# Both ends of a three-part transformer block: two blocks normalized on ScalarE, ternary weights by quarters, and first products placed in the end of attention

## The chip, the cores and the metric

The kernel runs on one core of a Trainium2 chip. The metric is device time in microseconds (us), the median of several runs. The engines are TensorE (PE for products, PEld for its weight loads), VectorE (DVE), ScalarE (ACT), GpSimd (POOL) and the DMA queues (SP and ACT issue here). Each engine works through its own instructions in order; it waits on semaphores for the others.

## The reference

Sixteen sequences of 256 tokens, 256 features: 4096 tokens. A feed-forward network with ternary weights, attention, and the same network again, each behind a layer norm without scale:

```python
def _bit_quant(w):
    scale = jnp.maximum(jnp.mean(jnp.abs(w)), EPS)
    w_ternary = jnp.clip(jnp.round(w / scale), -1.0, 1.0)
    ...
h = jnp.einsum('bsd,fd->bsf', x, w1q) + b1
h = jax.nn.gelu(h, approximate=False)
return jnp.einsum('bsf,df->bsd', h, w2q) + b2
...
x = x + 0.5 * _L0_ffn_ref(_layernorm(x, axis=-1), ...)
x = x + _L0_attn_ref(_layernorm(x, axis=-1), ...)      # 16 heads of 16, RoPE, causal softmax
x = x + 0.5 * _L0_ffn_ref(_layernorm(x, axis=-1), ...)
```

The ternary weight of w is 1 where w is above half the mean size, -1 where it is below minus half of it, else 0. So the thresholds need the whole matrix (its mean size), and the signs need the thresholds.

## The kernel before

All of x stays in SBUF: eight blocks of four tiles of 128 tokens (BT = 4, TB = 512). Every compute instruction goes through a wrapper (line 167) that keeps the order in which the program writes them on each engine, so this order is the schedule. A tile pool with a number of buffers makes an instruction that writes a buffer wait until all users of its last content are done, also those that are written further down.

**Feed-forward network.** ffn(ln, after) is used twice, with ln = 0 in front of attention and ln = 2 behind it. Its step(u) takes block i and feature slice f (128 of 1024 features) from u = 8 i + f. up(i, f) makes four products of 512 columns (the input is split into a high and a rest part, two halves of the 256 features each), then two Gelu passes on ACT (h_high, rounded, and h_whole, exact) and a subtraction h_rest on DVE, or on POOL where f is 1, 3 or 5. down(i, f) comes two steps later (LATE = 2): eight products into the block's output in PSUM. So PE's order is: up(u), then, in some steps, a turning of the next block, then down(u-2). prepare(i) normalizes a block (xn, one buffer), turn_in(i, k) transposes half of its features on PE, copies it to a rounded high part on ACT, and subtracts on DVE; both are written into the steps of the block before (f = 3, and f = 5 and 6).

**The start** (ln = 0, begin, lines 352 to 364): measure(0) takes the statistics of block 0 on DVE, finish_stats makes 1/sqrt(var) on POOL with a power; sizes(0) sums the sizes of w1, one half on DVE and one on ACT; prepare(0) normalizes on DVE; threshold(0) averages over the partitions with a product on PE and makes two thresholds on DVE; signs(0, half) makes ternary weights of half of w1 in two DVE instructions of 1024 elements; then turn_in(0, k), the other half of w1, and sizes(1) for w2, both halves on ACT. Step 0 makes w2's threshold and the first half of its signs, step 3 the second half; step 1 takes the statistics of block 1, step 3 normalizes it on DVE.

**Attention.** slot(b, p) is one of eight places of sequence b. In each place scores() makes, for two heads, eight products for the weights of sequence b-1 (tile w, in PSUM, two buffers) and eight for the row maxima of sequence b (tile m, maxima on DVE). weigh() adds the mask on DVE and takes the exponential on ACT into pT (five buffers). Other work is hung between: attend(b, half) multiplies pT with the values (32 products) and ACT copies the sums out; divide turns them back, turn_out transposes, project_out makes the output product, add_out adds to x, last_stats takes the statistics for the second network. turn_max(b, j) puts the row maxima in place with two small DMAs from SP's queue.

**The end of attention** (lines 733 to 771, a = 14, z = 15): eight places with the scores of the last sequence alone; `ahead` is put between a place's products and its mask, `behind` after its exponential. The first product of the second network is up(0, 0) in the loop behind. What is left of sequence 15 is `tail`, one part after each of the first five steps.

PSUM is full: two buffers of two banks for w and the network's output (ps_w), two of one bank for m and up's result (ps_m), two of one bank for all else (ps_mm, tiles mm).

Of the kernel before, what the change touches and what calls it, by code (L numbers as in the profile page):

```python
# [8 lines left out]
FP = mybir.dt.float32  # L9
FR = mybir.dt.float32r  # L10
AF = mybir.ActivationFunctionType
ALU = mybir.AluOpType
# [17 lines left out]
def kernel(  # L30
# [24 lines left out]
    fp = ctx.enter_context(tc.tile_pool(name="ffn", bufs=2))  # L55
    pp = ctx.enter_context(tc.tile_pool(name="proj", bufs=2))
    hp = ctx.enter_context(tc.tile_pool(name="heads", bufs=2))
    prp = ctx.enter_context(tc.tile_pool(name="probs", bufs=5))

# [148 lines left out]
    def sizes(n):  # L208
        for k in range(2):
# [4 lines left out]
            else:  # L214
# [58 lines left out]
    def ffn(ln, after):  # L273
        xn, xnT, hT, ys = {}, {}, {}, {}

        def measure(i):
            if ln == 0:
                for t in range(BT):
                    stats(0, i * BT + t)
                finish_stats(0, i * BT, BT)  # L280

        def prepare(i, engine=None):
            xn[i] = fp.tile([P, BT, D], FP, name="xn", bufs=1)
            for t in range(BT):
                normalize(ln, i * BT + t, xn[i][:, t, :], engine)
            xnT[i] = [fp.tile([P, KC, TB], FR, name=f"xnT_{n}") for n in range(2)]

        def add_bias(i):
# [9 lines left out]
            scalar.copy(high, tp)  # L298
            return lambda: vector.tensor_sub(rest, tp, high.bitcast(FP))

        def up(i, f):
            h = ps_m.tile([P, TB], FP, name="m")
            for n in range(2):
                for k in range(KC):
                    tensor.matmul(
                        h,
                        w1q[:, k, f * P : (f + 1) * P],
                        xnT[i][n][:, k, :],
                        start=(n == 0 and k == 0),
                        stop=(n == 1 and k == KC - 1),  # L310
                    )
            high = fp.tile([P, TB], FR, name="h_high", bufs=LATE + 3)
            rest = fp.tile([P, TB], FR, name="h_rest", bufs=LATE + 3)
            whole = fp.tile([P, TB], FP, name="h_whole", bufs=3)
            scalar.activation(high, h, AF.Gelu, bias=b1_sb[:, f : f + 1])
            scalar.activation(whole, h, AF.Gelu, bias=b1_sb[:, f : f + 1])

            engine = gpsimd if f in (1, 3, 5) and not (ln == 0 and i == NBLK - 1) else vector
            engine.tensor_sub(rest, whole, high.bitcast(FP))
            hT[i, f] = (high, rest)  # L320

        def down(i, f):
# [20 lines left out]
            if f == NFC - 1:  # L343
# [5 lines left out]
                for t in range(0, BT, 2):  # L349
                    after(i, t)  # L350

        def begin():
            measure(0)
            if ln == 0:
                sizes(0)
            prepare(0)
            if ln == 0:
                threshold(0)
                signs(0, lambda w: w[:, :, 0 : FF // 2])
            for k in range(KC):  # L360
                turn_in(0, k)()
            if ln == 0:
                signs(0, lambda w: w[:, :, FF // 2 :])
                sizes(1)

        def step(u):
            i, f = divmod(u, NFC)
            if i < NBLK:
                up(i, f)
                if ln == 0 and u == 0:  # L370
                    threshold(1)
                if ln == 0 and u in (0, 3):
# [6 lines left out]
                if ln == 0 and f >= 4 and i + 2 < NBLK:  # L379
# [3 lines left out]
                if i + 1 < NBLK:  # L383
                    if f == 3:
# [3 lines left out]
                if f == (1 if i == NBLK - 1 else 6):  # L388
# [8 lines left out]
        return begin, step, prepare, turn_in  # L397

    FFN_STEPS = NBLK * NFC + LATE

# [157 lines left out]

        return weigh if w is not None else lambda: None

    def attend(b, half):
# [14 lines left out]
        sums[b, half] = pp.tile([P, 2, S], FP, name="avs")  # L576
        scalar.copy(sums[b, half], av)

    def divide(b, half):
# [59 lines left out]
    def slot(b, p, more=lambda: None):  # L639
# [90 lines left out]

    begin, step, prepare, turn_in = ffn(2, store)
    rest = []
    for p in range(8):
        made = []
# [84 lines left out]
```

## Time and profile before

| | us |
|---|---|
| median of three runs (625.16 to 626.89) | 625.42 |
| the profiled execution | 622.22 |
| its span, first to last instruction | 620.4 |
| PE busy / DVE / ACT / POOL | 599.5 / 461.2 / 416.3 / 300.9 |
| first product on PE | 8.22 |
| first product of up(0, 0), ln = 0 | 11.75 |
| first product of down(0, 0), ln = 0 | 18.12 |
| down(0, 3), behind the first turning of block 1 | 25.35 |
| first place with sequence 15 alone | 468.46 |
| last exponential begins | 483.48 |
| up(0, 5), ln = 2 | 495.66 |

Times inside the profile are counted from the span's start. A group of instructions of one kind is printed in one line with its start, its length from the first start to the last end, and its number; the square bracket says how long the engine had been idle before and which engine's instruction let it go. A product's own time overlaps the next one's, so what a group costs PE is the distance from its start to the start of the next.

In the steady part of a network four up products take 0.93 us and eight down products 0.93 us, 1.87 us a step.

### The profile page before, as it was taken

How to read it: one execution, taken by the hardware profiler on the slowest of the kernel's cores; microseconds unless marked ns; L12 is line 12 of the kernel's file. 1: busy time of each engine (PE TensorE's matmuls, PEld its weight loads, DVE VectorE, ACT ScalarE, POOL GpSimd, SP SyncE). 2: the span in 40 equal slices, each digit the busy share in tenths (PEclk: the TensorE clock that was granted, in tenths of full speed). 3: DMA queues.
4: the chain of work that ended last, by engine and by line, in shares of the span. 5: the costliest groups of instructions: out<-in, count | busy, mean ns of one | idle time of the engine just before them, and what ended most of it. 6: DMA issues, size and time to landing. Idle time of an engine off the chain costs nothing.

```text
span 620.4 us, 14716 instructions
## 1 busy us (share of the span) xinstructions
PE 599.5 (97%) x5580; PEld 486.6 (78%) x5580; DVE 461.2 (74%) x1654; ACT 416.3 (67%) x716; POOL 300.9 (49%) x273
## 2 busy tenths in 40 slices
PE   4999999999999999999999999999998999999997
PEld 3798999887667777777777777777766798888886
DVE  6877777786788888888888888888886465555553
ACT  4666766664576677676777677767765676676674
POOL 3655555782464455545564456453430243334443
PEclk9999999999999999999999999999999999999999
DMA  8800000000001000100001000100100011011001
GB/s 285 180 22 1 2 1 18 17 1 18 20 35 38 19 21 36 38 27 29 19 36 38 20 20 36 37 20 21 36 4 2 1 35 35 34 35 35 27 21 55
DMA packets 25478, 21.30 MB, mean 34 GB/s; under 512 B 10944, under 2 KB 21056, under 8 KB 25408
## 3 DMA queue, kind: packets, MB, share of 16 engines
q1 hardware_dynamic: 24848, 19.44, 9.8%
q8 instruction: 44, 0.72, 0.5%
q10 hardware_dynamic: 560, 0.92, 0.4%
q14 instruction: 26, 0.21, 0.1%
HBM read 7.51 MB, written 4.19 MB: 19 GB/s over the span
## 4 chain that ended last, share of the span: by engine, by line
PE 89%; DVE 5%; ACT 3%; issue 1%; DMA 1%; POOL 1%; DVEq 0%; SPq 0%; POOLq 0%
PE mm L167 38%; PE w L167 29%; PE m L167 22%; DMA w<-in_w1T_dram 1%; DVE h_rest L167 1%; DVE xn L167 1%; ACT h_high L167 1%; ACT h_whole L167 1%; DVE w2q L167 1%; DVE st L167 1%; DVE w L167 0%; DVE x L167 0%; DVE masked L167 0%; DVE mv L167 0%; ACT pT L167 0%
## 5 line engine op out<-in xcount | busy, mean ns | idle before, releaser
L167 DVE CUSTOM_DVE_ANT_0 masked<-m,mask_q 128x128 f32<-128x128 f32 x480 | 142.7, 354 | 41.0 <-PE m L167 39.7
L167 PE MATMUL m<-xnT,w1q 128*128 128x512 f32 x512 | 145.1, 404 | 0.8 <-ACT xnT L167 0.7
L167 ACT ACTIVATE h_high<-m,b_sb 128x512 fp32r<-128x512 f32 x128 | 88.5, 691 | 78.2 <-PE m L167 78.1
L167 DVE TENSOR_TENSOR h_rest<-h_whole,h_high 128x512 fp32r<-128x512 f32 x83 | 75.0, 904 | 72.0 <-ACT h_whole L167 71.5
L167 ACT ACTIVATE pT<-w 128x768 f32<-128x768 f32 x128 | 104.1, 815 | 31.4 <-DVE w L167 24.9
L167 PE MATMUL w<-qT,kT 32*128 32x256 f32 (+1 forms) x1024 | 120.6, 348 | 1.9 <-ACT pT L167 1.8
L167 PE MATMUL w<-w2q,h_high 128*128 128x256 f32 x480 | 120.8, 285 | 0.7 <-DVE w2q L167 0.7
L167 PE MATMUL w<-w2q,h_rest 128*128 128x256 f32 x480 | 117.8, 279 | 0.4 <-POOL h_rest L167 0.3
L167 PEld LDWEIGHTS w<-qT,kT 32*128 32x128 f32 x1024 | 89.9, 184 | 33.0 <-issue 25.9
L167 PE MATMUL m<-kT,qT 32*128 32x128 f32 x960 | 114.9, 349 | 0.7 <-ACT kT L167 0.7
L167 POOL TENSOR_TENSOR h_rest<-h_whole,h_high 128x512 fp32r<-128x512 f32 x45 | 60.1, 1335 | 108.5 <-ACT h_whole L167 108.4
L167 PEld LDWEIGHTS m<-xnT,w1q 128*128 128x128 f32 x512 | 88.3, 190 | 16.7 <-DVE xnT L167 2.9
L167 PEld LDWEIGHTS w<-w2q,h_rest 128*128 128x128 f32 x480 | 90.4, 188 | 5.1 <-POOL h_rest L167 0.7
L167 PEld LDWEIGHTS w<-w2q,h_high 128*128 128x128 f32 x480 | 90.3, 188 | 5.2 <-DVE w2q L167 1.2
L167 DVE TENSOR_TENSOR w<-w,mask_k 128x512 f32<-128x512 f32 x128 | 88.8, 695 | 7.1 <-PE w L167 7.0
L167 ACT ACTIVATE h_whole<-m,b_sb 128x512 f32<-128x512 f32 x128 | 87.3, 682 | 0.0
L167 PEld LDWEIGHTS m<-kT,qT 32*128 32x128 f32 x960 | 65.9, 185 | 2.9 <-ACT kT L167 1.6
L167 POOL TENSOR_TENSOR w<-w,cosT 128x512 f32<-128x512 f32 x32 | 41.3, 1292 | 51.8 <-ACT w L167 31.9
L167 PE MATMUL mm<-xnT_a,wqk 128*128 128x256 f32 x256 | 62.2, 386 | 0.0
L167 POOL TENSOR_SCALAR var<-mv 128x4 f32<-128x4 f32 (+1 forms) x32 | 6.9, 216 | 106.2 <-DVE mv L167 105.6
L167 POOL TENSOR_TENSOR w<-w,sinT 128x512 f32<-128x512 f32 x32 | 41.0, 1280 | 26.0 <-DMA w<-w 25.9
L167 PEld LDWEIGHTS mm<-xnT_a,wqk 128*128 128x128 f32 x256 | 46.1, 190 | 7.6 <-issue 0.7
(86 smaller groups left out, 918.9 us busy)
## 6 DMA issues: line engine op xcount, KB each, us to landing
w<-w SPq DMA_DIRECT2D x64, 128.0 KB
out_dram<-x SPq DMA_DIRECT2D x15, 256.0 KB
x<-in_x_dram SPq DMA_DIRECT2D x7, 512.0 KB
w<-in_w2T_dram SPq DMA_DIRECT2D x1, 1024.0 KB
qT<-mT SPq DMA_DIRECT2D x64, 4.0 KB
w<-in_w1T_dram SPq DMA_DIRECT2D x1, 512.0 KB
w<-in_w1T_dram ACTq DMA_DIRECT2D x1, 512.0 KB
wqk<-in_wqkvT_dram SPq DMA_DIRECT2D x16, 32.0 KB
```

The costliest lines, as they stand in the source:

```text
L167: return tc.keep_in_program_order(getattr(self.engine, name)(*args, **kwargs))
```

## The change

1. **Pools.** pT has six buffers for five.
2. **Start, normalizing.** prepare(0) and prepare(1) of the first network run on ACT as Identity with scale rstd and bias `less` = -mean * rstd, which two small POOL instructions make. prepare(1) moves from step 3 to step 4, behind the last statistics of block 1.
3. **Start, signs.** Signs are made by quarters (512 elements) in place of halves. begin makes two quarters of w1; threshold(1) and w2's first quarter move into up(0, 0), between its Gelus and its subtraction; the other five quarters come in steps 1 to 5 (table `soon`), and between them the statistics of block 1, one tile each in steps 1 to 4.
4. **Start, PE.** turn_on(n) makes n products of the 128x128 matrix `averaging` with itself, that nothing uses: 20 in front of sizes(0), 4 behind the turning of block 0.
5. **Statistics of block 2** go from steps 4 to 7 to steps 8 and 9; the bias of block 0 is added at f = 7 instead of 6.
6. **End of attention.** up is split: up_first makes its products, up the rest. project_out(13) and add_out(13) move from the last slot into place 0; the other parts move to later places; block 1 of the second network is normalized on POOL in place 1 and turned in places 6 and 7; the products of up(0, 0) and up(0, 1) stand in places 3 and 5, those of up(0, 2) and up(0, 3) behind place 7, in a buffer of ps_w.
7. **Tail.** attend(15, 1) leaves its sums in PSUM; the copy comes one step later.

```diff
-    prp = ctx.enter_context(tc.tile_pool(name="probs", bufs=5))
+    prp = ctx.enter_context(tc.tile_pool(name="probs", bufs=6))
...
+    def turn_on(n):
+        on = ps_m.tile([P, P], FP, name="m")
+        for _ in range(n):
+            tensor.matmul(on, averaging, averaging, start=True, stop=True)
...
         def prepare(i, engine=None):
...
+            if engine is scalar:
+                less = small.tile([P, BT], FP, name="less")
+                gpsimd.tensor_scalar(less, mv[ln][:, at, 0], -1.0, 0.0, ALU.mult, ALU.add)
+                gpsimd.tensor_mul(less, less, rstd[ln][:, at])
...
+                    scalar.activation(
+                        xn[i][:, t, :],
+                        tokens(n),
+                        AF.Identity,
+                        bias=less[:, t : t + 1],
+                        scale=rstd[ln][:, n : n + 1],
+                    )
...
-        def up(i, f):
-            h = ps_m.tile([P, TB], FP, name="m")
+        first = {}
+
+        def up_first(i, f, to=None):
+            h = first[i, f] = ps_m.tile([P, TB], FP, name="m") if to is None else to
             for n in range(2):
                 for k in range(KC):
                     tensor.matmul(
...
+        def up(i, f):
+            if (i, f) not in first:
+                up_first(i, f)
+            h = first.pop((i, f))
...
             scalar.activation(whole, h, AF.Gelu, bias=b1_sb[:, f : f + 1])
+            if ln == 0 and (i, f) == (0, 0):
+                threshold(1)
+                signs(1, quarter(1, 0))
...
+        def quarter(n, k):
+
+            at = slice(2 * k * P, 2 * (k + 1) * P) if n == 0 else slice(2 * k, 2 * (k + 1))
+            return (lambda w: w[:, :, at]) if n == 0 else (lambda w: w[:, at, :])
...
+        soon = {
+            1: ((1, 1), 0),
+            2: ((0, 2), 1),
+            3: ((0, 3), 2),
+            4: ((1, 2), 3),
+            5: ((1, 3), None),
+        }
...
         def begin():
             measure(0)
-            if ln == 0:
-                sizes(0)
-            prepare(0)
-            if ln == 0:
-                threshold(0)
-                signs(0, lambda w: w[:, :, 0 : FF // 2])
+            turn_on(20)
+            sizes(0)
+            prepare(0, scalar)
+            threshold(0)
+            signs(0, quarter(0, 0))
             for k in range(KC):
                 turn_in(0, k)()
-            if ln == 0:
-                signs(0, lambda w: w[:, :, FF // 2 :])
-                sizes(1)
+            turn_on(4)
+            signs(0, quarter(0, 1))
+            sizes(1)
...
-                if ln == 0 and u == 0:
-                    threshold(1)
-                if ln == 0 and u in (0, 3):
-                    part = slice(0, NFC // 2) if u == 0 else slice(NFC // 2, NFC)
-                    signs(1, lambda w: w[:, part, :])
+                if ln == 0 and u in soon:
+                    part, t = soon[u]
+                    if u == BT:
+                        stats(0, BT + t)
+                        finish_stats(0, BT, BT)
+                        prepare(1, scalar)
+                    signs(part[0], quarter(*part))
+                    if u < BT:
+                        stats(0, BT + t)
...
-                if u == 1:
-                    measure(1)
...
+                if ln == 0 and u in (NFC, NFC + 1):
+
+                    for t in range(0, BT, 2):
+                        stats(0, 2 * BT + t + u - NFC)
+                    if u == NFC + 1:
+                        finish_stats(0, 2 * BT, BT)
...
-            if last is not None:
+            if last is not None and b < NB - 1:
                 project_out(last)
...
+    def take_sums(b, half):
+        av, sums[b, half] = sums[b, half], pp.tile([P, 2, S], FP, name="avs")
         scalar.copy(sums[b, half], av)
...
-    add_out(NB - 3)
     ahead = {
-        0: lambda: turn_max(z, 1),
-        6: lambda: project_out(a),
+        0: lambda: project_out(NB - 3),
+        1: lambda: turn_max(z, 1),
     }
     behind = {
-        0: lambda: attend(a, 1),
-        4: lambda: turn_out(a),
-        5: lambda: attend(z, 0),
-        2: lambda: (divide(a, 1), last_stats(NB - 3)),
-        7: lambda: (add_out(a), last_stats(a), divide(z, 0)),
+        0: lambda: add_out(NB - 3),
+        1: lambda: prepare(1, gpsimd),
+        2: lambda: attend(a, 1),
+        3: lambda: up_first(0, 0),
+        4: lambda: (divide(a, 1), last_stats(NB - 3)),
+        5: lambda: (up_first(0, 1), attend(z, 0)),
+        6: lambda: (turn_out(a), turn_in(1, 0)()),
+        7: lambda: (turn_in(1, 1)(), project_out(a), add_out(a), divide(z, 0), last_stats(a)),
     }
...
+    more = ps_w.tile([P, 2, TB], FP, name="w")
+    for f in range(2):
+        up_first(0, 2 + f, more[:, f, :])
     tail = [
-        lambda: attend(z, 1),
+        lambda: attend(z, 1, False),
+        lambda: take_sums(z, 1),
         lambda: divide(z, 1),
```

More of the change, by code (lines that the diff above doesn't have):

```diff
@@ L283, in prepare @@
             xn[i] = fp.tile([P, BT, D], FP, name="xn", bufs=1)
-            for t in range(BT):
-                normalize(ln, i * BT + t, xn[i][:, t, :], engine)
+            at = slice(i * BT, (i + 1) * BT)
+            if engine is scalar:
+                less = small.tile([P, BT], FP, name="less")
+                gpsimd.tensor_scalar(less, mv[ln][:, at, 0], -1.0, 0.0, ALU.mult, ALU.add)
+                gpsimd.tensor_mul(less, less, rstd[ln][:, at])
+            for t in range(BT):
+                n = i * BT + t
+                if engine is scalar:
+                    scalar.activation(
[5 more added lines that the diff above has]
+                    )
+                else:
+                    normalize(ln, n, xn[i][:, t, :], engine)
             xnT[i] = [fp.tile([P, KC, TB], FR, name=f"xnT_{n}") for n in range(2)]
@@ L369, in step @@
                 up(i, f)
-                if ln == 0 and u == 0:
-                    threshold(1)
-                if ln == 0 and u in (0, 3):
-                    part = slice(0, NFC // 2) if u == 0 else slice(NFC // 2, NFC)
-                    signs(1, lambda w: w[:, part, :])
+                if ln == 0 and u in soon:
[7 more added lines that the diff above has]
+                        stats(0, BT + t)
                 if ln == 0 and u == 4:
                     gpsimd.tensor_scalar(b2_sb, b2_sb, 0.5, 0.0, ALU.mult, ALU.add)
-                if u == 1:
-                    measure(1)
-                if ln == 0 and f >= 4 and i + 2 < NBLK:
+                if ln == 0 and u in (NFC, NFC + 1):
[3 more added lines that the diff above has]
+                        finish_stats(0, 2 * BT, BT)
+                if ln == 0 and f >= 4 and 0 < i and i + 2 < NBLK:
                     stats(0, (i + 2) * BT + f - 4)
@@ L382, in step @@
                         finish_stats(0, (i + 2) * BT, BT)
-                if i + 1 < NBLK:
-                    if f == 3:
+                if i + 1 < NBLK and (ln, i) != (2, 0):
+                    if f == 3 and (ln, i) != (0, 0):
                         prepare(i + 1)
@@ L387, in step @@
                         turn_in(i + 1, f - 5)()
-                if f == (1 if i == NBLK - 1 else 6):
+                if f == (1 if i == NBLK - 1 else 7 if ln == 0 and i == 0 else 6):
                     add_bias(i)
@@ L395, in step @@
                 later.pop(0)()
-        return begin, step, prepare, turn_in
+        return begin, step, prepare, turn_in, up_first
     FFN_STEPS = NBLK * NFC + LATE
@@ L559, in scores, with attend @@
         return weigh if w is not None else lambda: None
-    def attend(b, half):
+    def attend(b, half, take=True):
         av = ps_mm.tile([P, 2, S], FP, name="mm")
@@ L575, in attend @@
                     )
-        sums[b, half] = pp.tile([P, 2, S], FP, name="avs")
+        sums[b, half] = av
+        if take:
+            take_sums(b, half)
+    def take_sums(b, half):
+        av, sums[b, half] = sums[b, half], pp.tile([P, 2, S], FP, name="avs")
         scalar.copy(sums[b, half], av)
@@ L729, in store @@
             )
-    begin, step, prepare, turn_in = ffn(2, store)
+    begin, step, prepare, turn_in, up_first = ffn(2, store)
     rest = []
```

## The prediction

> **What bounds the kernel.** I read the page's busy times and its chain first, then PE's waits in the first 40 us and in the end of attention, then the timelines of DVE, POOL and ACT in these two stretches.
>
> ```profile
> PE 599.5 (97%) x5580; PEld 486.6 (78%) x5580; DVE 461.2 (74%) x1654; ACT 416.3 (67%) x716; POOL 300.9 (49%) x273
> PE 89%; DVE 5%; ACT 3%; issue 1%; DMA 1%; POOL 1%; DVEq 0%; SPq 0%; POOLq 0%
> ```
>
> PE sets the time; 620.4 - 599.5 = 20.9 us are without a product. Whatever makes PE wait anywhere is paid in full, and a part moved on another engine counts only by PE's waits. At the start PE waits little once it runs:
>
> ```profile
> PE w L167 <- DVE w2q L167: 0.7, 1, 0.7
> PE m L167 <- ACT xnT L167: 0.7, 1, 0.7
> PE mm L167 <- DVE xn L167: 0.2, 1, 0.2
> ```
>
> What the reader is to see next is DVE's order behind it. Block 1's statistics (the last at 20.03) come before the second half of w2's signs (20.70 and 21.49), the power on POOL runs beside that half, and block 1 is normalized at 22.69, just when PE has done up(5):
>
> ```profile
> 20.03 0.18 DVE L167 BATCH_NORM_AGGREGATE mv<-st 128x2 f32<-128x6 f32 x1
> 20.13 0.66 DVE L167 TENSOR_TENSOR h_rest<-h_whole,h_high 128x512 fp32r<-128x512 f32 x1
> 20.70 0.75 DVE L167 TENSOR_SCALAR w2q<-w,half 128x1024 fp32r<-128x1024 f32 x1
> 21.49 1.28 DVE L167 SCALAR_TENSOR_TENSOR w2q<-w,half,w2q 128x1024 fp32r<-128x1024 f32 x1
> 22.69 2.52 DVE L167 TENSOR_SCALAR xn<-x,mv,rstd 128x256 f32<-128x256 f32 x4
> ```
> ```profile
> 20.92 1.40 POOL L167 TENSOR_TENSOR rstd<-var,power 128x4 f32<-128x4 f32 x1
> 22.29 1.64 POOL L167 TENSOR_TENSOR h_rest<-h_whole,h_high 128x512 fp32r<-128x512 f32 x1
> ```
>
> The end of attention loses 2.7 us of PE to waits:
>
> ```profile
> PE w L167 <- ACT pT L167: 1.8, 2, 1.1
> PE mm L167 <- ACT avs L167: 0.6, 1, 0.6
> PE mm L167 <- DVE xnT L167: 0.3, 1, 0.3
> ```
> ```profile
> 468.46 0.92 PE L167 MATMUL w<-qT,kT 32*128 32x256 f32 x8
> 469.31 0.44 PE L167 MATMUL mm<-ident,maxes 128*128 128x128 f32 x2
> 469.68 1.51 PE L167 MATMUL mm<-pT,vals 128*32 128x256 f32 x32
> 471.12 0.95 PE L167 MATMUL w<-qT,kT 32*128 32x256 f32 x16
> 472.00 0.66 PE L167 MATMUL mm<-ident,avs 128*128 128x128 f32 x4
> ```
>
> The eight products of one place hold PE 0.85 us (468.46 to 469.31), the sixteen of two places side by side 0.88 (471.12 to 472.00): neighbours overlap.
>
> **Start, up to step 0.** Normalizing on ACT: nearest row is kT (Identity with bias and scale from memory, 128x256), 595 ns, with the next instruction 0.10 before its end, so 0.49 apart. ACT's size pass over w1 and its accumulator read end at 8.25; `less` on POOL (two small ones, 0.2 each like var, behind rstd's 7.66) is ready then. Four passes end at 10.35 (DVE's ended at 9.37). Transposes, two copies of 0.59: 11.9, before 11.63. sizes(1), 2.2 us: 14.1, before 13.72. So w2's threshold and the first Gelus come 0.3 us later, and w2's `half` is ready at 14.9. turn_on(20): nearest are the project_out products, eight in 1.9 us for 256 columns; half of that for 128, twice it at the speed of the first products (below): 40 instructions take 4.8 to 9.5 us from 1.1 us. At worst threshold(0) is 2.3 us late; its first quarter would be ready at 12.5 instead of 10.2, and the subtraction that up(0, 0) needs anyway ends at 12.6. That cover makes it free; without it up to 2.3 us would be paid. I take 0, and 0 for turn_on(4), which lies in front of the same subtraction.
>
> **Start, DVE's list.** A quarter: the comparison of 512 elements lies between 0.40 (256) and 0.75 (1024), the second instruction like other two-input ones of 512, 0.68; together 1.15 (bounds 1.02, half of the rows above, and 1.3). The statistics of a tile take 0.53, a subtraction 0.62. From 14.9: w2's quarter 16.05, rest(0) 16.7 (down(0) starts here, 1.4 before the old 18.12), w2's second 17.8, statistics 18.35, rest(2) 19.0, w1's third 20.1, statistics 20.65, w1's fourth 21.8, statistics 22.3, rest(4) 23.2 (it waits for Gelu 4, whose products wait for w1's third quarter), last statistics 23.75. Before: 20.21. The cause is that 2.3 us of w1's signs, which DVE did up to 14.78 while w2's sizes were being summed, now stand in front of block 1's statistics.
>
> POOL makes it worse. The first of the four normalizations at 22.69 waited for POOL's subtraction (22.29 to 23.93): the four took 2.52 us, against 1.37 at 7.99 with POOL idle, 1.15 more. Two POOL subtractions (f = 1 and 3) now fall into this list: 0 to 2.3 us, I take 1.4: 25.15.
>
> Behind it: var and power (1.3 us alone, 2.1 beside DVE's signs at 20.30 to 22.32), two small `less` (0.2 to 0.4 each, with a 0.1 step each): 1.8 to 3.0, I take 2.2. Then four ACT passes, 2.1, in front of which Gelu 5 queues: 29.45. PE finished up(5) at about 24 and stands in turn_in(1, 0), with down(3) and all steps behind it. down(3) starts at 29.6; before, 25.35. **Loss +4.2 us**; bounds +1.5 (no contention, quarters at 1.02, ACT passes 0.40 apart) and +5.8. Nothing hides it: after 25.35 PE hardly waits.
>
> The earlier down(0) and the faster up products are lost in that wait. Statistics at steps 8 and 9 put 1.1 us on DVE in a step of 1.87, ahead of a use three steps later: 0. The bias one step later is wanted at step 9: 0.
>
> **The clock.** Four up products take 2.05 us at 11.75 and 1.09 at 19.17 (0.43 and 0.23 each): PE starts slow. The page "TensorE: Matmul & The Clock Gate" (Part 1) of the Trainium skill says that PE drops to half speed after an idle window of about 3.4 us. No wait between products before shows it, since all are shorter; by the rule the new wait of some 5 us, with four transposes in it, could start it, and the steps behind would pay, as an estimate from that window, 2 to 3 us more; without it, nothing.
>
> **End of attention.** PE's order with its own rows (place 0.86, attend 1.44, transposes 0.42, project_out 1.9 at 479.79 to 481.71, up 0.93): place 0 at 466.8, project_out(13), place 1 at 469.45, maxima, place 2 at 470.7, attend(14, 1), place 3 at 473.0, up(0, 0), place 4 at 474.75, divide, place 5 at 476.05, up(0, 1), attend(15, 0), place 6 at 479.25, turn_out, turn_in, place 7 at 481.0. The old waits are filled. A mask starts 1.04 after its place, its exponential 0.73 later. The third pT of sequence 15 needs a buffer that attend(14, 1), written behind it, still reads: its exponential slips from 472.45 to 473.1, and place 4 doesn't need it before 474.75. turn_max's two DMAs (SP has no others here) go from place 0 to place 1, three places ahead of their reader, as in each slot before: 0. Normalizing block 1 on POOL, 4 x 1.22 (its rows at 453 to 457), ends at 475.3, five us ahead of its turning, and last_stats queues behind without harm: 0.
>
> Then new waits. ACT copies turn_out and turn_in behind exponential 6 (to 482.33 and 482.9), DVE subtracts until 483.6; place 7's mask queues behind this subtraction. PE waits for a mm buffer 0.5 before the second turning and 0.85 before project_out(14), and 0.9 before divide(15, 0), whose buffer hangs on a copy behind the last exponential (to 486.3). The table load (1.28) and Gelus 0 to 2 lie beside up(0, 2), up(0, 3), attend and down; but turn_out(15) waits 0.95 for divide's DVE part, which stands behind rest(2). Sum 3.2 us of new waits for 2.7 of old. Followed to the end, up(0, 5) starts at 497.4; before 495.66, and two turnings of 0.44 were still to come: 496.54. **Loss +0.9 us.** Bounds: no new wait, -2.7 and +0.8 for the pair that no longer overlaps, -1.9; the table load uncovered as well, +2.2.
>
> **Sum.** The profiled execution's 622.22 + 4.2 + 0.9 = 627.3; it lies 3.2 below the median shown, so against the runs **630.5**. By the bounds 625.0 to 633.4.
>
> **Rivals.** (a) *PE goes half-speed again in the new wait*: the first slow stretch lasts from 8.22 to 16.5, of which half is lost where PE is full: 0 to 4.1, I take 2.5: 633.0. For it: the wait's length; against: transposes in it. Chance 0.28. (b) *The start works as meant*: block 1 is normalized before PE asks, the 1.4 us of the earlier down(0) stay, and the end fills its waits (-1.9): 622.1. It decides if the last statistics end by 19.5; DVE would have to shed 4 us. For it: the ACT list is short; chance 0.12. (c) *Both at their good bounds*, +1.5 and -1.9: 625.0, no change; 0.06. (d) The forecast, a wait of PE in front of block 1's turning: 0.54.
>
> **Range and chances.** 626.0 and below needs (b) or (c), 634.5 and above the dear half of (a). I give 625.5 to 634.5. This kernel's measurement tells 0.3%, 1.9 us: faster 0.12, same 0.06, slower 0.82.
>
> **What would show it.** Right: PE waits once for 3 to 6 us on ACT's xn near 24 to 30; down(0) starts near 16.7; last block-1 statistics near 24 to 26; in the end, waits of mm products on DVE's xnT near 483 to 486 and none of w on pT. Products of 0.43 us each behind the wait show (a). Wrong: statistics by 20, or block 1 turned without a wait.

## The result, and the profile after

| | before | after |
|---|---|---|
| median, us | 626.15 (4 runs, 625.16 to 627.00) | 633.41 (4 runs, 632.99 to 633.75) |
| ratio, 95% interval | | 1.0126 [1.0099, 1.0153] |
| profiled execution / its span | 622.22 / 620.4 | 633.30 / 631.5 |
| mean granted clock in that execution | 1.000 | 0.990 |

The change costs 7.3 us against the runs. Between the two profiled executions it is 11.1 us; the two differences part because the old kernel was profiled in one of its quickest executions, and why that matters is the second half of this story. The same marks in both traces show where the 11.1 us lie:

| first product of, or start of | before | after | later by |
|---|---|---|---|
| down(0, 0), first network | 18.12 | 16.16 | -1.96 |
| down(0, 2) | 21.97 | 23.86 | 1.89 |
| down(0, 3) | 25.35 | 31.61 | 6.26 |
| down(1, 7) | 49.14 | 57.42 | 8.28 |
| first exponential | 167.78 | 176.49 | 8.71 |
| last exponential of sequence 14 | 468.30 | 477.09 | 8.79 |
| down(0, 5), second network | 501.21 | 511.55 | 10.34 |
| end of the span | 620.43 | 631.51 | 11.09 |

So 8.3 us in the start, 1.55 in the end of attention (10.34 - 8.79), and 1.25 that creep in where the program is the same, 0.5 before 477 us and 0.75 behind 511.

The busy times of the page after, and the shares of its chain:

```profile
PE 612.1 (97%) x5628; PEld 496.8 (79%) x5628; DVE 458.3 (73%) x1650; ACT 419.2 (66%) x724; POOL 305.7 (48%) x281
PE 87%; DVE 5%; ACT 3%; issue 1%; POOL 1%; DVEq 0%; POOLq 0%; ACTq 0%
```

PE has 48 more instructions and 12.6 us more of busy time (599.5 before). The 48 are turn_on's 24 products, two instructions each: the first forty hold PE from 1.12 for 6.49 us, the last eight for 0.8. The other 5.3 us are products that took longer. PE's waits in the first 40 us, after (total, times, longest):

```profile
PE mm L167 <- ACT xn L167: 4.2, 5, 3.4
PE m L167 <- DVE w1q L167: 2.4, 1, 2.4
```

The first is the wait that was predicted. The second is up(0, 4), which waits for the third quarter of w1's signs; the prediction has it only as a small delay on DVE's list, not as a wait of PE. The chain of waits after (start, length, what) runs through both:

```profile
20.24 1.64 DVE w1q L167
21.89 0.14 issue
22.02 2.06 PE m L167 x4
...
25.40 0.69 DVE h_rest L167
26.09 0.35 DVE st L167
...
27.15 1.52 POOL rstd L167
...
29.12 0.21 POOL less L167
...
29.36 0.61 ACT xn L167
```

Signs, products, a subtraction behind their Gelus, the last statistics of block 1, the power on POOL, `less`, ACT's pass, and only then the turning. The stretches of the start after (length, then busy time and number of PE, PEld, DVE, ACT and POOL, then granted clock, DMA share, GB/s):

```profile
18.50:22.00 3.50, 1.09 (x9) 0.89 (x8) 3.43 (x7) 1.27 (x2) 1.31 (x1) 0.99 1.15 322
22.00:25.40 3.40, 3.38 (x12) 3.01 (x13) 2.04 (x6) 1.26 (x2) 0.00 (x0) 0.51 0.49 48
25.40:28.70 3.30, 1.16 (x6) 0.63 (x5) 3.19 (x7) 0.00 (x0) 1.86 (x2) 1.00 0.73 93
28.70:35.50 6.80, 5.44 (x18) 4.07 (x19) 0.98 (x2) 3.78 (x8) 3.71 (x5) 0.50 0.42 64
```

Each of the two waits is followed by products at half speed: 3.4 us behind the first, 6.8 behind the second. The four products at 22.02 take 2.04 us. In the end of attention PE's waits after are:

```profile
PE mm L167 <- DVE xnT L167: 1.3, 2, 0.7
PE mm L167 <- DVE o L167: 0.5, 1, 0.5
PE w L167 <- ACT pT L167: 0.5, 1, 0.5
```

The places wait little for pT now (none was forecast; 0.5 came, in front of place 0), and the turnings wait for DVE instead.

### The profile page after: what moved, and what is told of

It is laid out like the page before. It is cut to its first block, busy times and chain, and to the rows that moved or that the text cites. A ratio compares the mean times of both kernels' runs of the same rounds, so it can differ in the third digit from the quotient of the medians.

```text
span 631.5 us, 14831 instructions
## 1 busy us (share of the span) xinstructions
PE 612.1 (97%) x5628; PEld 496.8 (79%) x5628; DVE 458.3 (73%) x1650; ACT 419.2 (66%) x724; POOL 305.7 (48%) x281
## 4 chain that ended last, share of the span: by engine, by line
PE 87%; DVE 5%; ACT 3%; issue 1%; POOL 1%; DVEq 0%; POOLq 0%; ACTq 0%
PE mm L167 37%; PE w L167 29%; PE m L167 22%; DVE h_rest L167 1%; ACT h_whole L167 1%; ACT h_high L167 1%; DVE xn L167 1%; DVE w2q L167 1%; POOL rstd L167 0%; DVE x L167 0%; ACT pT L167 0%; DVE st L167 0%; DVE masked L167 0%; DVE w1q L167 0%; DVE w L167 0%
## 5 line engine op out<-in xcount | busy, mean ns | idle before, releaser
L167 PE MATMUL m<-xnT,w1q 128*128 128x512 f32 x504 | 143.1, 404 | 2.4 <-DVE w1q L167 2.4
L167 ACT ACTIVATE h_high<-m,b_sb 128x512 fp32r<-128x512 f32 x126 | 86.7, 688 | 81.6 <-PE m L167 81.6
L167 DVE TENSOR_TENSOR h_rest<-h_whole,h_high 128x512 fp32r<-128x512 f32 x83 | 73.7, 888 | 76.9 <-ACT h_whole L167 76.5
L167 PE MATMUL w<-w2q,h_high 128*128 128x256 f32 x480 | 123.3, 289 | 0.0
L167 PE MATMUL w<-w2q,h_rest 128*128 128x256 f32 x480 | 120.8, 284 | 0.4 <-POOL h_rest L167 0.3
L167 PEld LDWEIGHTS w<-w2q,h_high 128*128 128x128 f32 x480 | 91.9, 192 | 4.7 <-issue 0.5
L167 ACT ACTIVATE h_whole<-m,b_sb 128x512 f32<-128x512 f32 x126 | 85.8, 681 | 0.0
```

Source lines behind the costliest of these rows:

```text
L167: return tc.keep_in_program_order(getattr(self.engine, name)(*args, **kwargs))
```

## The experiments

Three questions stand open. Which end costs what; whether the start's loss is the order on DVE, the passes on ACT, the new products on PE or the clock; and where the 1.25 us come from that no edit touches. Every ratio is to the kernel before, run beside it. "Later by" is counted as in the table above, at down(1, 7) for the start.

**One end at a time, and the old kernel once more.** The start alone keeps the old end and five pT buffers; the end alone keeps the old start:

```diff
 # the start alone, against after
-    prp = ctx.enter_context(tc.tile_pool(name="probs", bufs=6))
+    prp = ctx.enter_context(tc.tile_pool(name="probs", bufs=5))
...
+    add_out(NB - 3)
     ahead = {
-        0: lambda: project_out(NB - 3),
-        1: lambda: turn_max(z, 1),
+        0: lambda: turn_max(z, 1),
+        6: lambda: project_out(a),
...
 # the end alone, against before: ahead, behind, tail and up_first as in the change
```

> The changed start with the old end of attention (five pT buffers, turning of block 1 in the loop). Theory (the loss is PE's wait in front of block 1's turning, with half-speed products behind it): 5 to 7 us slower than before, down(3) at 30 to 32 us in the profile, half-speed products behind it. Rival (the end of attention holds most of the loss): not more than 3 us slower.

> The changed end of attention alone, with the old start. Theory (new waits for mm buffers take the place of the filled ones): 0.5 to 2 us slower than before, PE waits on DVE's xnT between 480 and 486. Rival (the products placed there fill PE's waits): 1 to 2.5 us faster.

> The kernel before, once more, for a second profile. The profiled execution of it took 622.22 us, 3.9 below the median of its timed runs. If the moment at which PE becomes fast differs from run to run, this profile shows down(3) later than 25.35 with the products before it at 0.43 us each; if the 3.9 us lie elsewhere, the start is the same and the networks' steps are longer than 1.87 us.

The start alone takes 632.65 us, ratio 1.0137 [1.0102, 1.0172]; down(0, 3) begins at 31.70. It is 7.4 over before's median here, a little more than the 5 to 7 expected, and carries the loss, the creeping 1.3 us too (8.68 later at down(1, 7), 9.94 at the end). The end alone takes 623.81, 0.9977 [0.9958, 0.9995]: 0.5 to 2 us slower had been expected, and it is *not* slower but 1.5 faster than the median of before. Yet against the first profile of before its trace is 1.59 us later at down(0, 5), which is the 1.55 of the change. Both are true, and the third run shows how. The old kernel again took 624.97, with a span of 623.2, and lost its 2.8 us in one place, the end of attention. This is that stretch in the first execution of before:

```profile
472.00:475.60 3.60, 2.50 (x27) 2.04 (x24) 3.34 (x9) 1.51 (x2) 0.28 (x2) 1.00 0.02 5
475.60:482.40 6.80, 6.12 (x68) 4.47 (x66) 2.14 (x4) 4.10 (x6) 0.64 (x1) 1.00 0.00 0
```

and in the second:

```profile
472.00:475.60 3.60, 2.50 (x30) 1.94 (x23) 3.23 (x9) 1.51 (x2) 0.19 (x1) 1.00 0.02 6
475.60:482.40 6.80, 6.45 (x52) 4.14 (x51) 1.54 (x3) 3.39 (x5) 0.72 (x1) 0.50 0.00 0
```

The same program, the same 2.50 us of PE busy in the 3.6 before, and then clock 1.00 in one execution and 0.50 in the other: 68 products against 52.

The trace records when the granted clock changes. In all fourteen traces the recorded changes lie whole multiples of 3.413 us apart (1, 2, 3, 5 and so on up to 180 of them; only the last record is cut off by the end of the trace). But these marks don't fall on the same places of the program: in the first execution they are at 470.44 and 473.85, in the second at 472.19 and 475.60. So the stretch between two marks was not the same one. That this parted the two is not shown: the stretch from 470.44 in the first and the one from 472.19 in the second both hold 2.31 us of products, and only the second was followed by half speed. Each run lists its mean clock, so the 77 runs of the old kernel that the experiments brought can be laid out by it:

| mean granted clock | runs | median us | from, to |
|---|---|---|---|
| 0.998 to 1.000 | 13 | 622.3 | 622.13, 622.96 |
| 0.996 | 16 | 623.9 | 623.69, 624.76 |
| 0.993, 0.994 | 19 | 625.1 | 624.76, 625.38 |
| 0.990 | 29 | 626.9 | 626.52, 627.62 |

A stretch of 3.4 us at half speed lowers the mean over 622 us by 0.0027 (3.4 / 2 / 622). The mean also counts the last us of the span, where the clock falls behind the last products (in the changed kernel from 629.5 on). So the steps stand, roughly, for none, one, two (the second profile: 6.8 us, 0.994) and three. The median of before (625.1 to 626.5 in these sets) is an execution that has lost 3 to 4 us to the clock; the first profile is one that lost none.

**Is that loss a matter of PE's gaps?** Before's order, with seven products that nothing uses put into the gaps of its end:

```diff
-        4: lambda: turn_out(a),
+        4: lambda: (turn_out(a), turn_on(3)),
...
-        2: lambda: (divide(a, 1), last_stats(NB - 3)),
+        2: lambda: (divide(a, 1), turn_on(4), last_stats(NB - 3)),
```

> The kernel before, with seven products that nothing uses in the two waits of PE in the end of attention (four behind divide in place 2, three behind turn_out in place 4). Theory (in some executions of the kernel before PE falls to half speed there, as in its second profile from 475.6 to 482.4, and 2.7 us are lost): no execution near 626, all within 0.5 us, at 622 to 623. Rival (the scatter has another cause): scatter and median as before, about 625.

It took 622.39 us, all twelve runs between 622.24 and 622.87, ratio 0.9958 [0.9944, 0.9971]. The scatter of before (622.1 to 627.6) is gone and its lowest time is the rule, by seven products of 128 columns. That settles it for the old end.

**The start's loss: order, ACT, products or clock.** Four kernels, each the changed one with one thing different. The order: block 1's statistics all in step 1 and its normalization in step 3, as before, both ahead of these steps' quarters of signs:

```diff
+                if ln == 0 and u == 1:
+                    measure(1)
+                if ln == 0 and u == 3:
+                    prepare(1, scalar)
                 if ln == 0 and u in soon:
-                    part, t = soon[u]
...
-                        prepare(1, scalar)
-                    signs(part[0], quarter(*part))
-                    if u < BT:
-                        stats(0, BT + t)
+                    signs(soon[u][0][0], quarter(*soon[u][0]))
```

> The changed kernel, but block 1's statistics all in step 1 and its normalization (still on ScalarE) in step 3, ahead of the quarters of steps 1 to 5; nothing else changed. Theory (DVE's order is the cause): last statistics near 18.7 us, down(3) at 24.5 to 26.5, no half-speed products behind it, 5 to 8 us faster than the changed kernel, so 625 to 628. Rival (normalizing on ScalarE or the quarters themselves cost the time): down(3) stays at 29 or later, less than 3 us faster than the changed kernel.

628.44 us, 1.0063 [1.0041, 1.0086]: the earlier place of the statistics gives 5.0 us back. That is the order and the half speed that goes with it, together. down(0, 3) begins at 27.75, later than expected, and half speed isn't gone, as had been expected; one stretch is left of three. Its waits of PE show why, and the second view the stretch:

```profile
PE m L167 <- DVE w1q L167: 3.1, 1, 3.1
PE mm L167 <- ACT xn L167: 0.8, 4, 0.3
```
```profile
23.40:26.80 3.40, 3.40 (x14) 3.02 (x13) 1.02 (x2) 3.13 (x6) 0.25 (x1) 0.50 0.57 58
```

The wait for xn is nearly gone, and the one for w1's third quarter has grown. Put first, statistics delay signs; put last, signs delay statistics: DVE has too much in front of step 4. The old order made the second half of w1's signs while w2's sizes were summed, and its waits in the first 40 us have no line for w1's signs.

The passes: blocks 0 and 1 normalized on DVE again, all else as changed.

```diff
-            prepare(0, scalar)
+            prepare(0)
...
-                        prepare(1, scalar)
+                        prepare(1)
```

> The changed kernel with blocks 0 and 1 normalized on VectorE again, at the places where ScalarE did it; all else as changed. Theory (ScalarE's four passes take 2.1 us and two small POOL instructions stand in front, VectorE's take 1.4 and none): 1 to 2.5 us faster than the changed kernel, and still a wait of PE over 2 us in front of block 1's turning. Rival (moving the normalization off VectorE is the cause): 5 us or more faster. Other rival (VectorE is the scarce engine, so ScalarE relieves it): slower.

631.85 us, 1.0108 [1.0081, 1.0135], but not by a shorter start: it is 8.8 later at down(1, 7), as DVE's four passes now meet POOL's subtraction and, behind it, the addition of the bias to block 0:

```profile
26.73 4.53 DVE L167 TENSOR_SCALAR xn<-x,mv,rstd 128x256 f32<-128x256 f32 x4 [1.41 <-POOL rstd L167]
```
```profile
27.15 1.29 POOL L167 TENSOR_TENSOR h_rest<-h_whole,h_high 128x512 fp32r<-128x512 f32 x1
28.41 2.39 POOL L167 TENSOR_TENSOR x<-x,b_sb 128x1024 f32<-128x1024 f32 x1
```

4.53 us where they took 1.37 with POOL idle; ACT's passes are the better half of the change. What this kernel gains it gains behind the start: the creep is gone (8.78 later at down(1, 7), 8.71 at the last exponential of sequence 14, and 10.24 at down(0, 5) of the second network and at the end). It has no tile `less`; that leads to the test below.

The products of turn_on taken away:

```diff
-            turn_on(20)
...
-            turn_on(4)
```

> The changed kernel without its 24 turn_on products. Theory of the prediction (they are free and of no use, since DVE's list decides): within 1 us of the changed kernel. Rival (they make the first steps faster and that counts): 1 us or more slower.

633.39 us, 1.0134 [1.0103, 1.0164], against 633.41 with them: nothing. They are not the loss and save none of it. The two starts differ all the same. Without them PE is granted the full clock only from 19.1 (4.8 with them), and down(0, 0) begins at 18.71 (16.16). But with these slow first steps up(0, 4) doesn't wait for w1's signs, and the first stretch at half speed doesn't come; down(0, 3) begins at 31.33 (31.61). What the products win in the first steps is lost again in the waits behind.

The clock: products that nothing uses in the two waits.

```diff
+                    if ln == 0 and u == 5:
+                        turn_on(14)
                     if f in (5, 6):
...
                 down(*divmod(u - LATE, NFC))
+            if ln == 0 and u == 3:
+                turn_on(9)
```

> The changed kernel with PE kept at work in its two waits at the start: nine more turn_on products behind down(1), fourteen between up(5) and the first turning of block 1; they use nothing that the rest needs. Theory (the half-speed stretches at 21.9 and 28.7 us are on the path and cost 2.5 to 4 us of the loss): no products of 0.43 us left behind 10 us, down(3) near 30.5 instead of 31.6, 2.5 to 4 us faster than the changed kernel, so 629.5 to 631. Rival (DVE's order costs all of it, the clock only fills a wait): within 1 us of the changed kernel.

631.92 us, 1.0112 [1.0085, 1.0139]. The start is 6.1 later in place of 8.3, so half speed costs 2.1 to 2.2 us there, if anything more: w2's threshold comes 0.42 later in this execution than in the changed kernel, ahead of both waits. That is less than the 2.5 to 4 expected. Only 1.5 of it shows in the median, because two of its four runs lost some clock elsewhere (mean 0.995 and 0.997 with 632.7, 0.998 and 1.000 with 631.2). Its profile is one of them; the start is at full clock, and then in the changed end:

```profile
28.70:35.50 6.80, 5.44 (x33) 4.48 (x34) 1.55 (x2) 5.43 (x10) 3.83 (x4) 1.00 0.54 75
```
```profile
471.00:474.40 3.40, 2.86 (x29) 1.87 (x27) 3.40 (x19) 1.40 (x2) 2.84 (x3) 1.00 0.02 5
474.40:477.80 3.40, 3.40 (x8) 2.39 (x8) 1.67 (x3) 1.62 (x2) 2.00 (x2) 0.50 0.00 0
```

In the first line PE has 33 products where the changed kernel had 18, in the same 5.44 us of busy time.

**The creep.** The old kernel with its end kept warm, and one small unused tile in the pool that holds `less`:

```diff
+    less = small.tile([P, BT], FP, name="less")
+    nc.gpsimd.memset(less, 0.0)
```

> e_tail_warm (622.4) with one tile more that nothing reads, `less`, in the pool of small tiles, as the changed kernel has it; one memset of it on GpSimd at the start. In the profiles of the changed kernel the distance to the kernel before grows by 0.4 us along the first network and 0.6 along the second (products of down follow 117 to 124 ns apart instead of 113 to 120), and it doesn't where normalization went back to VectorE and the tile is gone. Theory (the tile moves what lies behind it in SBUF, and that costs some ns a product): 0.8 to 1.3 us slower than e_tail_warm, steps of down drift by about as much. Rival (the drift comes with the work on ScalarE): within 0.3 us.

623.73 us (623.5 to 623.92) against 622.39 (622.24 to 622.87) without it: 1.34 us for a tile that nothing reads. (The two ran on different chips; the kernel before at full clock took 622.2 to 622.4 beside the first and 622.4 to 623.0 beside the second, so the chip isn't the cause.) In the trace 0.42 us of it lie in the first network, 0.7 in the second, none in attention. The down products of the second network, from 505 to 600 us, first without the tile, then with it (busy time, mean ns):

```profile
L167 PE MATMUL w<-w2q,h_rest 128*128 128x256 f32 x189 | 46.3, 278 | 0.0
```
```profile
L169 PE MATMUL w<-w2q,h_rest 128*128 128x256 f32 x188 | 46.8, 282 | 0.0
```

4 ns a product here; those with h_high take 286 for 285. The six kernels of this document with `less` in the pool of small tiles all show 282 ns in that stretch; the eight without it, or with it in the last pool (the two last ones), show 278 or 279. So it is shown that this tile in this pool makes the creep, and that work on ScalarE doesn't. That it acts by the addresses of what is allocated behind it is inferred from the pool's place in front of the large ones; what it is about those addresses was not tried and stays open.

**A version that beats both.** The end first: project_out(13) goes back to the last slot, up(0, 2) and up(0, 3) move ahead of place 7's mask, the turning's subtractions go behind that mask and behind project_out(14), last_stats(14) goes to the tail, and the subtraction of slice 2 to POOL.

```diff
     ahead = {
-        0: lambda: project_out(NB - 3),
         1: lambda: turn_max(z, 1),
+        7: lambda: ups_ahead(),
     }
...
-        6: lambda: (turn_out(a), turn_in(1, 0)()),
-        7: lambda: (turn_in(1, 1)(), project_out(a), add_out(a), divide(z, 0), last_stats(a)),
+        6: lambda: (turn_out(a), held.append(turn_in(1, 0))),
+        7: lambda: (held.pop()(), held.append(turn_in(1, 1)), project_out(a), held.pop()(), add_out(a), divide(z, 0)),
...
```

> e_end_only (old start, changed end; 623.8) with its new waits taken away: project_out(13) back in the last slot, up(0, 2) and up(0, 3) between place 7's products and its mask, the two subtractions of block 1's turning behind that mask and behind project_out(14), last_stats(14) three steps later, the rest of slice 2 on GpSimd. Theory (PE waits for mm buffers and for DVE's list are what the changed end loses): 1.5 to 2.5 us faster than e_end_only, so 621.3 to 622.3. Rival (the loss is in the places that no longer overlap in pairs): within 0.5 us of e_end_only.

With the old start it took 622.07 us, 0.9967 [0.9946, 0.9988], 1.7 less than the changed end alone. PE's waits from 460 to 505 us:

```profile
PE w L167 <- ACT pT L167: 0.6, 1, 0.6
PE mm L167 <- DVE x L167: 0.4, 1, 0.4
PE mm L167 <- DVE xnT L167: 0.3, 1, 0.3
```

1.3 us in all. Three of its twelve runs had a mean clock of 0.997 and took 623.5 to 623.8, the others 621.9 to 622.3 at 0.998 to 1.000; where those three lost the clock was not profiled.

Then the start, with the old end kept warm: three quarters of w1's signs before step 0 (two in the change, all four in the old order), one tile's statistics there too and the other three in step 1, `less` in the last pool.

```diff
             signs(0, quarter(0, 0))
+            signs(0, quarter(0, 1))
             for k in range(KC):
                 turn_in(0, k)()
             turn_on(4)
-            signs(0, quarter(0, 1))
+            signs(0, quarter(0, 2))
             sizes(1)
+            stats(0, BT)
...
+        soon = {1: (1, 1), 2: (0, 3), 3: (1, 2), 4: (1, 3)}
...
```

> The old end with its two waits filled (e_tail_warm, 622.4), and a start that keeps ScalarE's normalization and the quarters but orders DVE by who waits first: three quarters of w1 before w2's threshold, block 1's statistics right behind rest(0), its normalization in step 3; `less` lies in the last pool. Theory (DVE's order, not the quarters or ScalarE, made the loss): down(3) at 23 to 25 instead of 25.35, no half-speed products behind 10 us, 0.5 to 2.5 us faster than e_tail_warm. Rival (quarters on DVE beside POOL's subtractions cost more than the order gives): down(3) behind 26, slower than e_tail_warm.

down(0, 3) begins at 25.08 (25.35 before), and the median is 623.14, 0.9984 [0.9965, 1.0003]: 0.75 more than the warm old end takes with the old start, where 0.5 to 2.5 less had been expected. Ten of its twelve runs have a mean clock of 0.994 to 0.997; where they lose it isn't known, as the profiled one (622.36) is at 1.000. PE still waits 2.0 us for xn, and POOL's timeline says why:

```profile
19.02 1.69 POOL L167 TENSOR_TENSOR rstd<-var,power 128x4 f32<-128x4 f32 x1
20.52 1.31 POOL L167 TENSOR_TENSOR h_rest<-h_whole,h_high 128x512 fp32r<-128x512 f32 x1
21.91 0.52 POOL L167 TENSOR_SCALAR less<-mv 128x4 f32<-128x4 f32 x1
```

`less` is written in step 3 and so stands behind step 3's subtraction: it starts 1.4 us after that does (21.91 and 20.52). Last, both together, with `less` made right behind the power, in step 1, and three more products in place 1 of the new end:

```diff
+                    finish_stats(0, BT, BT)
+                    shift(1)
                 if ln == 0 and u == 3:
                     prepare(1, scalar)
...
```

> The reordered start of e_new_start with the reordered end of e_new_end; the two GpSimd instructions of `less` for block 1 move ahead of the subtraction of slice 3, where the profile of e_new_start shows them 1.4 us behind the power; three products that nothing uses fill PE's wait in place 2. Theory (both ends lose by order alone): down(3) near 24, the end as in e_new_end, 619.5 to 621.5, faster than the kernel before by more than 3 us. Rival (the start stays limited by DVE's list): down(3) at 25, 621.5 to 622.5.

620.83 us (twelve runs, 620.61 to 621.91), ratio 0.9934 [0.9911, 0.9957]: ahead of the kernel before, and of all others here. down(0, 3) begins at 23.84. Its span and clock, and what PE still waits for ACT in the first 45 us:

```profile
core 0: 618.9 us, clock 1.000
```
```profile
PE mm L167 <- ACT xn L167: 1.0, 6, 0.2
```

Against before's executions at full clock (622.3) it is 1.6 us shorter, of which 1.3 are the start; the rest of the 5.7 us between the medians (626.52 for before, run beside it) is clock that it mostly doesn't lose: its slowest run takes 621.91. The later statistics of block 2 and the sixth pT buffer were not tried alone; both are in this kernel.

## Why the prediction was right, and where not

The forecast (d), a wait of PE in front of block 1's turning, is what happened, and the measured 633.4 lies in the range and beside rival (a). But the sum came as near as 2.9 us by errors that partly cancel, which is luck: 5.1 us against the profiled execution, where 11.1 came, and an offset of 3.2 that the changed kernel doesn't have.

*Right.* The place, and the order on DVE as its cause: the kernel with the old order of statistics gives 5.0 us back, clock included. down(0, 0) earlier (16.16; 16.7 was put). turn_on at nothing. ACT's four passes 2.07 us (2.1 put). The four new waits of the end stand where they were put, and are shorter: 0.3, 0.6, 0.7 and 0.5 us for 0.5, 0.85, 0.9 and 0.95. Rival (b), the start as meant, is out: the last statistics ended at 26.64.

*The start's loss, mis-sized by 2.0 us at down(0, 3).* 4.2 were put, with 5.8 as the dear bound; 6.26 came, and 5.78 with PE kept at work in the waits. 1.5 of the 2.0 are DVE's list: the end of the last statistics was forecast at 25.15 and measured at 26.64 (26.46 + 0.18). Where it went can be read on DVE after:

```profile
17.00 1.68 DVE L167 SCALAR_TENSOR_TENSOR w2q<-w,half,w2q 128x512 fp32r<-128x512 f32 x1
...
20.24 1.63 DVE L167 SCALAR_TENSOR_TENSOR w1q<-w,half,w1q 128x512 fp32r<-128x512 f32 x1
...
22.84 0.75 DVE L167 SCALAR_TENSOR_TENSOR w1q<-w,half,w1q 128x512 fp32r<-128x512 f32 x1
...
25.40 0.69 DVE L167 TENSOR_TENSOR h_rest<-h_whole,h_high 128x512 fp32r<-128x512 f32 x1 [1.26 <-ACT h_whole L167]
...
26.46 0.18 DVE L167 BATCH_NORM_AGGREGATE mv<-st 128x2 f32<-128x6 f32 x1
```

The first two took 0.9 us longer than the third, each beside one of POOL's subtractions:

```profile
16.77 1.36 POOL L167 TENSOR_TENSOR h_rest<-h_whole,h_high 128x512 fp32r<-128x512 f32 x1 [8.55 <-ACT h_whole L167]
...
20.02 1.31 POOL L167 TENSOR_TENSOR h_rest<-h_whole,h_high 128x512 fp32r<-128x512 f32 x1 [1.89 <-ACT h_whole L167]
```

DVE's instructions end 0.55 behind POOL's (18.68 and 18.13; 21.87 and 21.33), as if most of their work had been done only when POOL was through. A page of the Trainium skill has a reason ("SBUF — State Buffer", section "SBUF: two separate sides"): the port pair that VectorE and GpSimd share is held for a whole instruction, and the other engine stands still; a VectorE instruction with two inputs in SBUF takes part against a GpSimd one that reads SBUF. These two rows, which have such inputs, are in line with it but for some 0.2 us (0.55 behind POOL's end, 0.75 alone). They cost 1.8 us, where I took 1.4. The other part is the 1.26 us that DVE waits in front of rest(4): I had written that up(0, 4) waits for w1's third quarter and charged DVE's list some 0.3 us for it. But those products ran at half speed, Gelu 4 came late, and rest(4), ahead of the last statistics on DVE, with it. In the kernel with products in the waits, at full clock, the same wait of DVE is 0.39. POOL then took 2.6 us from var to `less`, where 2.2 was put.

*The clock, weighed as a rival, not as the forecast.* It was given 0.28 and 2.5 us; it came, and cost 2.1 to 2.2 us in the start, by the kernel with products in the waits. The step that failed is "no wait between products before shows it, since all are shorter". The page "TensorE: Matmul & The Clock Gate" (Part 1) of the Trainium skill names an idle window of about 3.4 us, and I took it as wholly idle. The traces don't bear that out: the 3.5 us before the first half-speed stretch hold 1.09 us of products, the 3.4 in the old end's second execution 2.31. The wait of 2.44 on w1's signs sufficed, in a place where the sum had no wait of PE.

*The end of attention.* +0.9 against the profiled execution; +1.55 came. Counted back by the 8.79 that the stretch starts late, place 0 begins at 466.80 and place 3 at 473.08 (466.8 and 473.0 were put), but place 7 at 481.78, 0.8 late. PE's timeline after shows one cause, up(0, 0) and the place behind it:

```profile
482.72 1.20 PE L167 MATMUL m<-xnT,w1q 128*128 128x512 f32 x4
483.85 0.92 PE L167 MATMUL w<-qT,kT 32*128 32x256 f32 x8
```

Four up products between places hold PE 1.13 us, not the 0.93 of the steady part; four transposes take 0.59 there, not 0.42. The waits give 1.05 back; some 0.9 more lies behind place 7 (the eight products of up(0, 2) and up(0, 3) take 2.04 for 1.86) and wasn't followed row by row. The sign of the term against the runs is wrong: the changed end alone is 1.5 us *faster* than the median of before, as the old end loses 1.6 to 4.6 us to the clock in 64 of 77 runs and the changed one in one of ten.

*The offset.* "It lies 3.2 below the median shown, so against the runs 630.5" took the difference as something that every kernel carries along. It was the old end's loss of clock, which the change took away. Set against before at full clock, the parts read in the traces are 6.1 for the start, 2.15 for its clock, 1.55 for the end, 1.25 for the creep, 11.05 in all; 622.3 + 11.05 = 633.35, and the median measured is 633.41. Without the wrong offset my sum would have said 627.3.

*The creep* of 1.25 us was in no term: a tile of 4 numbers a partition, in a pool that keeps four of each.

## What to carry to other kernels

When runs of one kernel scatter in steps, lay them out by their mean clock before pricing a change from one profile: the profiled execution may be one that escaped a loss that most pay, and a change can win or lose by that alone. On an engine that works in order, count everything that stands in front of the instruction that another engine's start hangs on; splitting work into smaller parts helps only if the part that is wanted first also stands first, and DVE work of the kinds held up here (signs with two inputs, 0.75 to 1.68 us; four normalizations, 1.37 to 2.52 and 4.53) should be counted at nearly the sum of both when it meets GpSimd's. Where PE must wait for a few us, some products that nothing uses cost nothing measurable in these runs and kept it at speed there.

## What the runs showed of the hardware that was not expected

Half speed came in stretches of 3.4 us and multiples of it: 3.4 and 6.8 in the changed kernel, 6.8 in the old one, and 10.3 with the passes on DVE, where this line holds the clock 0.50 from 26.9 to 37.2:

```profile
26.90:37.20 10.30, 7.15 (x27) 5.93 (x28) 7.91 (x11) 2.33 (x4) 3.89 (x3) 0.50 0.40 55
```

The stretch before need not be idle: PE was busy for 31% of it (1.09 of 3.5 us) in the changed kernel's start, for 68% (2.31 of 3.41) in the old end, and for 84% (2.86 of 3.4) in the changed end of the kernel with products in the waits, where 24 of the 29 products have 32 rows. Nor does the share alone decide: with the passes on DVE, the stretch from 20.15 to 23.57 held 1.99 us, 58%, and full speed followed; and 2.31 us did and didn't bring half speed in two executions of one program. How much work such a stretch needs stays open. And one small tile in a pool ahead of others made the products with h_rest 4 ns longer, 278 to 282, and the kernel 1.34 us.
